# Query products as three rounded passes in one bank, grouped output weights added in transfer, weight checks over three stages

## The chip, the cores and the metric

The kernel runs on one core of a Trainium2 chip. The metric is the device time of one execution in microseconds; the kernel before takes 470.77 us, the median of three runs (470.35 to 471.19).

## The reference

Two layers on a batch of 2 × 512 rows of 512 values. Each of the four steps adds to its input and normalises over the row (layernorm). Cut to the first layer, which the change touches:

```python
q = (x @ Wq.T + bq).reshape(b, s, 32, 128)
sig_q = elu(q) + 1.0
q_sel = sig_q[:, :, ::4, :]                       # 8 of 32 heads are used
num = einsum('bshd,hde->bshe', q_sel, M)
den = einsum('bshd,hd->bsh', q_sel, z)[..., None] + 1e-6
out_heads = repeat(num / den, 4, axis=2)          # each head stands for 4
x = layernorm(x + out_heads.reshape(b, s, 4096) @ Wo.T)
xf = x / 128.0                                    # feed-forward, 1376 wide
inter = silu(xf @ w_gate.T) * (xf @ w_up.T)
inter_q = trunc(clip(inter * 128.0, -128.0, 127.0))
down = trunc(clip((inter_q @ w_down.T) * 128.0, -128.0, 127.0))
x = layernorm(x + down)
```

The feed-forward weights of this layer hold one magnitude with a sign, or zero. The second layer is a one-head attention and a gated feed-forward of the same width with ordinary weights.

## The kernel before, in words

**Stages.** Activations lie in eight row tiles of 128 × 512, four for each batch. The first layer has a query stage, a read stage, a gate-and-up stage and a down stage; the second follows.

**Query stage** (`queries`, L379). For each batch and each of 8 heads, `query_products` multiplies four 128-row blocks of the head's weights with the transposed rows in FP32 into one PSUM bank. ScalarE takes exp (L388) and relu (L390) from it, VectorE joins both into `q` (L392), of which sixteen stay in memory. Batch 0 goes first, head by head, then batch 1. The first product follows its rows tile by tile (`first_queries`, L368).

**Output weights.** As four output heads repeat one read head, their four 128 × 512 weight blocks can be summed. `wo` comes as two halves of two blocks for each head (L332) into six rooms of 512 KiB (`wop`). `sum_weights` (L404) adds the halves and then the two blocks, half of the heads on POOL and half on VectorE. `fold` (L412) multiplies the turned memory M with the sum; ScalarE writes the result, less its last column, to `mw` (L416, L417). The last column of `mw` holds `z`.

**Read stage** (`read`, L419). For each of eight row tiles, eight FP32 products of `q` with `mw` (L428) fill the eight PSUM banks. ScalarE takes the denominators (L432), VectorE inverts them; three heads leave over ScalarE (`y`, L441) and POOL (L445), five over VectorE (L450). The row tile is then normalised (`norm_a0`), cut into two rounded parts (`split`), and for batch 1 turned by squares and transfers.

**Weight checks.** To multiply with signs alone, the kernel divides the gate and up weights by their largest magnitude (`ternary`, ScalarE, L463) and counts on VectorE where sign times magnitude differs from the weight (`compare`, L210). There are 22 such checks (`check_up`): 15 from the fourth head of batch 1 on, seven in the first three tiles of the read stage. The sum (`total`, after the fourth tile) and the verdict (`verdict`, after the fifth) give a flag. TensorE loads it into a register (`branch`, L235) and each product of the next stage branches on it. For the products the weights are divided again into rooms of their own (`divided`), in the last six tiles of the read stage.

**Gate-and-up stage** (`up`, L604). For each batch and each of 11 chunks of the width, 16 rounded passes fill two banks (L611). ScalarE and VectorE turn them into the truncated middle values. Chunk c + 6 is divided when chunk c of batch 1 is through, into the room that this leaves (`to_divide`). The down weights are checked beside it in the same way, with POOL dividing (`check_down`, L465).

**Order.** Each engine has one instruction list; the framework orders it by its own estimates, `issue_after` pins single steps, and POOL's order is as written. Loads stand in SP's queue in the order written; a load whose room is in use holds up those behind it. `pair_tile` and `query_tile` rooms are reused by later stages.

Of the kernel before, what the change touches and what calls it, by code (L numbers as in the profile page):

```python
# [19 lines left out]
P = 128  # L20
# [12 lines left out]
LENT = 3  # L33
TOP12 = -4096
# [4 lines left out]
def kernel(  # L39
# [179 lines left out]
    def verdict(tot, sc, name):  # L219

        k = sc.shape[-1]
        pf = psum(f"pf_{name}")
        nc.tensor.matmul(pf[:, :1], ones, tot, start=True, stop=True)
        yes = small.tile([P, 1], F32, tag="yes", name=f"yes_{name}", bufs=1)
        nc.vector.tensor_scalar(yes, pf[:, :1], 0.0, None, ALU.is_equal)
        no = small.tile([P, 1], F32, tag="no", name=f"no_{name}", bufs=1)
        nc.vector.tensor_scalar(no, pf[:, :1], 0.0, None, ALU.not_equal)
        flag = const.tile([1, 1], I32, tag=f"flag_{name}", name=f"flag_{name}")
        nc.vector.tensor_copy(flag, yes[0:1, 0:1])
        eff = const.tile([P, k], F32, tag=f"eff_{name}", name=f"eff_{name}")  # L230
        nc.vector.tensor_scalar(eff, sc, yes, no, ALU.mult, ALU.add)
        return flag, eff
# [65 lines left out]
    wop = ctx.enter_context(tc.tile_pool(name="wop", bufs=6))  # L298

    def pair_tile(name):  # L300
        return wop.tile([P, 2, HID], F32, tag="wo", name=name)

    wqp = ctx.enter_context(tc.tile_pool(name="wqp", bufs=4))

    def query_tile(name):
        return wqp.tile([P, 2, HID], F32, tag="wq", name=name)

    with tc.tile_pool(name="a0w", bufs=1) as a0w, tc.tile_pool(name="a0", bufs=2) as a0:
# [12 lines left out]
        load_x(1)  # L321
# [4 lines left out]
        for h in range(NH):  # L326
            halves = []
            if h == 6:
                gus = up_weights(gu0_in, "0", range(1))
            for j in range(2):  # L330
                w = pair_tile(f"wo{h}_{j}")
                nc.sync.dma_start(w, wo0_in[h, :, ts(j, G // 2), :])  # L332
                halves.append(w)
            wos.append(halves)

        gus += up_weights(gu0_in, "0", range(1, len(CHUNKS)))
        nc.sync.dma_start(wqkv, wqkv_in.rearrange("(k p) f -> p k f", p=P))
        bqk = const.tile([D, 3], F32, tag="bqk", name="bqk")
        nc.sync.dma_start(bqk, bqk_in)
        nc.sync.dma_start(bv, bv_in.to_broadcast([P, D]))  # L340
        nc.sync.dma_start(wo1, wo1_in)
        nc.sync.dma_start(bo, bo_in.to_broadcast([P, HID]))

        mw = a0w.tile([D, NH, HID], F32, tag="mw", name="mw")
        nc.gpsimd.tensor_copy(mw[:, :, LAST], z)

        def query_products(pq, xt, h, at):  # L350
            for k in range(NK):
                done = nc.tensor.matmul(  # L352
                    pq[:, at], wq[h][:, k, :], xt[:, k, at],
                    start=(k == 0), stop=(k == NK - 1),
                )
            return done

        def first_rows(xt, t):
# [5 lines left out]
            nc.scalar.copy(xt[:, :2, ts(t, P)], pt[:, :2])  # L364
            nc.vector.tensor_copy(xt[:, 2:, ts(t, P)], pt[:, 2:])
            return done

        def first_queries(pq, xt):  # L368

            done = first_rows(xt, 0)  # L370
            for t in range(NT):
                if t + 1 < NT:
                    with tc.issue_after(done.ins):
                        done = first_rows(xt, t + 1)
                with tc.issue_after(done.ins):
                    done = query_products(pq, xt, 0, ts(t, P))
            return done

        def queries(b, xt, h):  # L379

            pq = psum(f"pq_{b}_{h}")
            if b == h == 0:
                done = first_queries(pq, xt)
            else:
                done = query_products(pq, xt, h, slice(0, S))

            e = a0.tile([D, S], F32, tag="e", name=f"e_{b}_{h}")
            nc.scalar.activation(e, pq, AF.Exp, bias=bq[:, h : h + 1])  # L388
            r = a0.tile([D, S], F32, tag="r", name=f"r_{b}_{h}")
            nc.scalar.activation(r, pq, AF.Relu, bias=bq[:, h : h + 1])  # L390
            q = a0.tile([D, S], F32, tag="q", name=f"q_{b}_{h}", bufs=16)
            nc.vector.scalar_tensor_tensor(q, e, 1.0, r, ALU.min, ALU.add)  # L392
            qs[b].append(q)
            return done
# [9 lines left out]
        def sum_weights(eng, h):  # L404

            w, w1 = wos[h]
            eng.tensor_add(w, w, w1)
# [52 lines left out]
        def ternary(eng, out, w, factor):  # L460

            if eng is nc.scalar:
                eng.activation(out, w, AF.Copy, scale=factor)  # L463
            else:
                eng.tensor_scalar(out, w, factor, None, ALU.mult)  # L465

        counts = const.tile([P, 2 * len(CHUNKS)], F32, tag="counts", name="counts")

        def check_up(c, a):
            n = CHUNKS[c][1]  # L470
            w = gus[c][:, a].rearrange("p k i -> p (k i)")
            t = a0.tile([P, NK * P], F32R, tag="t", name=f"t_{c}_{a}")
            ternary(nc.scalar, t[:, : NK * n], w, inv_up[:, a : a + 1])
            junk = a0.tile([P, NK * P], I8, tag="junk", name=f"junk_{c}_{a}", bufs=1)
            i = 2 * c + a
            compare(
                junk[:, : NK * n], t[:, : NK * n].bitcast(F32), w,
                sc_up[:, a : a + 1], counts[:, i : i + 1],
            )

        checks = [(c, a) for c in range(len(CHUNKS)) for a in range(2)]
        qs = [[], []]
        xt = xtp.tile([P, NK, S], F32, tag="xt", name="xt_a00")
        with tc.issue_after(queries(0, xt, 0).ins):
            queries(0, xt, 1)
        for h in range(2, NH):
            queries(0, xt, h)
            if h == 4:
                sum_weights(nc.gpsimd, 0)
                turn_memory()  # L490
                sum_weights(nc.vector, 1)
            elif h == 6:
                xt1 = transposed(xs[1], "a01")
                sum_weights(nc.vector, 2)
        sum_weights(nc.gpsimd, 3)
        for h in range(NH):
            queries(1, xt1, h)
            if h == 0:
                sum_weights(nc.vector, 4)
                sum_weights(nc.gpsimd, 5)  # L500
                fold(0)
                fold(1)
                with tc.issue_after(copies[-1].ins):
                    mx_up = largest(
                        [gus[0][:, a].rearrange("p k i -> p (k i)") for a in range(2)], "up"
                    )
            elif h == 1:
                top_up = over_partitions(mx_up, "up")
            elif h == 2:
                sc_up, inv_up = scales(top_up, "up")  # L510
                fold(2)
                fold(3)
                sum_weights(nc.vector, 6)
                sum_weights(nc.gpsimd, 7)
            elif h == 3:
                fold(4)
            elif h == 5:
                fold(5)
                fold(6)
            elif h == 6:  # L520
                fold(7)
            if h >= 3:
                for _ in range(3):
                    check_up(*checks.pop(0))
        order = [(b, t) for b in range(B) for t in range(NT)]
# [11 lines left out]
        def divided(c, a):  # L537
            n = CHUNKS[c][1]
            if c not in ts_up:
                t = (pair_tile if c in PAIRED else query_tile)(f"tu_{c}").bitcast(F32R)  # L540
                ts_up[c] = t.rearrange("p a (k i) -> p a k i", k=NK)
                if n < P:
                    nc.gpsimd.memset(ts_up[c][:, :, :, n:].bitcast(F32), 0.0)
            ternary(nc.scalar, ts_up[c][:, a, :, :n], gus[c][:, a], inv_up[:, a : a + 1])

        PAIRED = (LEAD - 2, LEAD - 1, len(CHUNKS) - 1)
        ts_up, x2 = {}, []
# [5 lines left out]
        for i, (b, t) in enumerate(order):  # L553
            steps = read(b, t, lambda steps: norm_a0(i - 1, steps) if i else None)
            for _ in range((3, 2, 2, 0, 0, 0, 0, 0)[i]):
                check_up(*checks.pop(0))
            if i == 3:
                tot_up = total(counts, "up")
            elif i == 4:
                flag_up, eff_up = verdict(tot_up, sc_up, "up")  # L560
            if i >= len(order) - LEAD:
                for a in range(2):
                    divided(i - len(order) + LEAD, a)
# [30 lines left out]
    with tc.tile_pool(name="f0", bufs=2) as f0:  # L594
        ternary_up = branch(flag_up)
        silu_scale = const.tile([P, 1], F32, tag="silu_scale", name="silu_scale")
        nc.vector.tensor_scalar(silu_scale, eff_up[:, 0:1], 1.0 / 128.0, None, ALU.mult)
# [6 lines left out]
        def up(b, c, behind=()):  # L604
            n = CHUNKS[c][1]
            t = ts_up[c]
            pp = [psum(f"pg_f0{b}_{c}"), psum(f"pu_f0{b}_{c}")]
# [33 lines left out]
            for part in to_divide.get((b, c), ()):  # L641
                divided(*part)
# [83 lines left out]
        step = up(1, 0)  # L726
        with tc.issue_after(step.ins):
            mx_d = largest([wds[0]], "down")
        up(1, 1)
        last = len(CHUNKS) - 1  # L730
        for c in range(LEAD, last + 1):
            up(0, c)
            if c == LEAD:
                top_d = over_partitions(mx_d, "down")
# [586 lines left out]
```

## Time and profile before

| | |
|---|---|
| median of three runs | 470.77 us (470.35 to 471.19) |
| profiled execution, first to last instruction | 468.7 us |
| median less that span | 2.1 us |
| query stage, to the first read product | 0 to about 72 us |
| read stage | 72 to 130.65 us |
| gate-and-up stage, to the first down product | 130.65 to 208.4 us |
| ScalarE busy, 24.5 to 72.3 us | 32.95 of 47.8 us |
| VectorE busy, 24.5 to 72.3 us | 30.68 of 47.8 us |
| transfers, 4.6 to 24.5 us | 356 GB/s, 98% of the engines' time |
| `wo` load, 512 KiB, issue to landing | 6.9 us (median of 16) |

The profiled execution's own time is known as its span; what lies around it is the difference in the third line. PE is TensorE's products, PEld its weight loads, DVE VectorE, ACT ScalarE, POOL GpSimd and SP the queue that issues most loads. A row of the view in order of time gives the start, the length, the engine, the line, the operation with output and inputs, the shape and the count. The length of consecutive instructions of one kind overlaps, so the distance from start to start is their rate. A bracket at the end names idle time before it and what ended that.

### The profile page before, as it was taken

The numbers are of one execution on the slowest core, as the hardware profiler recorded it, in microseconds if no ns is written. First come the engines' busy times: TensorE is split into PE (matmuls) and PEld (weight loads), VectorE is DVE, ScalarE is ACT, GpSimd is POOL, SyncE is SP. The second block draws the span as 40 slices with busy tenths as digits, with TensorE's granted clock in tenths as the row PEclk, the third lists the DMA queues.
The fourth block names the chain that finished last, engine by engine and source line by source line (L and its number), as shares of the span: only waits on it lengthen the run. The fifth ranks groups of instructions, "written<-read, shape, count | busy, mean of one in ns | idle before, by whom it ended". The sixth has DMA issues, their size and how long they took to land.

```text
span 468.7 us, 5727 instructions
## 1 busy us (share of the span) xinstructions
PE 461.0 (98%) x1883; PEld 329.0 (70%) x1883; DVE 329.5 (70%) x627; ACT 267.5 (57%) x507; POOL 115.1 (25%) x144
## 2 busy tenths in 40 slices
PE   9999999999999999999999999999999999999994
PEld 8454444434478888888866567888888888888884
DVE  1165677767876767775979889895755778998632
ACT  3344799557756767456756842584645768443101
POOL 0235101566543053600357032000000000050111
PEclk9999999999999999999999999999999999999999
DMA  8989900000006500051390000000000000001001
GB/s 284 381 297 363 387 9 0 0 0 3 1 1 134 201 1 3 11 162 45 91 390 31 0 1 1 1 0 1 1 0 1 0 1 1 1 24 45 37 31 45
DMA packets 21651, 35.02 MB, mean 75 GB/s; under 512 B 9840, under 2 KB 10736, under 8 KB 21616
## 3 DMA queue, kind: packets, MB, share of 16 engines
q1 hardware_dynamic: 19616, 33.73, 20.7%
q10 hardware_dynamic: 1872, 0.56, 0.5%
q8 instruction: 22, 0.36, 0.3%
q0 software_dynamic: 128, 0.26, 0.3%
q14 instruction: 13, 0.11, 0.1%
HBM read 31.40 MB, written 2.10 MB: 71 GB/s over the span
## 4 chain that ended last, share of the span: by engine, by line
PE 71%; ACT 7%; DVE 5%; issue 3%; POOL 0%; POOLq 0%; DVEq 0%; ACTq 0%
PE pm L1111 17%; PE pg_f L611 9%; PE pu_f L611 9%; PE pc L1111 8%; PE pdm L1199 7%; PE pd_f L666 4%; PE pdc L1199 4%; DVE x L450 3%; PE pqk L893 3%; PE po L428 2%; ACT y L441 2%; ACT t L463 2%; PE pv L906 2%; PE pot L989 1%; PE po L1005 1%
## 5 line engine op out<-in xcount | busy, mean ns | idle before, releaser
L428 PE MATMUL po<-mw,q 128*128 128x512 f32 x128 | 57.1, 598 | 0.3 <-DVE mv_a L139 0.2
L352 PE MATMUL pq<-xt_a,wq 128*128 128x512 f32 (+1 forms) x152 | 56.9, 526 | 0.0
L145 POOL TENSOR_TENSOR rstd_f<-mv_f,ln_eps 128x1 f32<-128x1 f32 x15 | 4.4, 293 | 169.3 <-DVE mv_f L1214 130.2
L428 PEld LDWEIGHTS po<-mw,q 128*128 128x128 f32 x128 | 22.9, 189 | 32.1 <-issue 17.7
L352 PEld LDWEIGHTS pq<-xt_a,wq 128*128 128x128 f32 x152 | 26.2, 190 | 27.4 <-issue 25.7
L1111 PE MATMUL pm<-r,ugu 128*128 128x512 f32 x152 | 37.7, 389 | 0.0
L1111 PE MATMUL pm<-r,it_early 128*128 128x512 f32 x144 | 36.7, 392 | 0.0
L1111 PEld LDWEIGHTS pm<-r,ugu 128*128 128x128 f32 x152 | 28.5, 188 | 5.9
L1111 PEld LDWEIGHTS pm<-r,it_early 128*128 128x128 f32 x144 | 27.0, 188 | 6.1 <-issue 0.5
L169 ACT ACTIVATE ta_f<-y_f,below_half 128x512 int8<-128x512 f32 (+1 forms) x22 | 15.9, 721 | 27.0 <-DVE y_f L157 26.7
L450 DVE SCALAR_TENSOR_TENSOR x<-po,den,x 128x511 f32<-128x511 f32 x40 | 29.8, 745 | 1.9
L1121 DVE SCALAR_TENSOR_TENSOR ev_q<-pm,ev_q 128x512 f32<-128x512 f32 x27 | 18.6, 688 | 14.4 <-PE pm L1111 14.4
L637 DVE SCALAR_TENSOR_TENSOR it_f<-tb_f,ta_f 128x512 fp32r<-128x512 int16 (+1 forms) x22 | 15.4, 702 | 18.3 <-ACT tb_f L170 18.3
L445 POOL TENSOR_TENSOR y<-y,y 128x511 f32<-128x511 f32 x16 | 20.3, 1271 | 31.5 <-ACT y L441 30.8
L388 ACT ACTIVATE e<-pq,bq 128x512 f32<-128x512 f32 x16 | 11.1, 692 | 24.1 <-PE pq L352 20.6
L611 PE MATMUL pg_f<-xh,tu 128*128 128x512 f32 x88 | 24.3, 398 | 0.0
L1120 ACT ACTIVATE ev_q<-pc 128x512 f32<-128x512 f32 x27 | 16.0, 593 | 14.2 <-PE pc L1111 14.1
L465 POOL TENSOR_SCALAR td<-wd,inv_down 128x512 fp32r<-128x512 f32 x11 | 18.2, 1668 | 22.1 <-DVE inv_down L205 22.1
L611 PE MATMUL pg_f<-xl,tu 128*128 128x512 f32 x88 | 23.6, 390 | 0.0
L611 PE MATMUL pu_f<-xh,tu 128*128 128x512 f32 x88 | 23.5, 389 | 0.0
L611 PE MATMUL pu_f<-xl,tu 128*128 128x512 f32 x88 | 23.5, 389 | 0.0
L1001 ACT ACTIVATE x<-x,off_f,rstd_f 128x512 f32<-128x512 f32 x7 | 5.7, 816 | 27.7 <-POOL off_f L1000 27.7
(315 smaller groups left out, 1087.5 us busy)
## 6 DMA issues: line engine op xcount, KB each, us to landing
gu<-in_gu SPq DMA_DIRECT2D x20, 512.0 KB, 7.9
wo<-in_wo SPq DMA_DIRECT2D x16, 512.0 KB, 6.9
wd<-in_wd SPq DMA_DIRECT2D x20, 256.0 KB, 4.5
wq<-in_wq SPq DMA_DIRECT2D x8, 256.0 KB, 4.9
x<-in_x SPq DMA_DIRECT2D x7, 256.0 KB, 5.4
out<-x SPq DMA_DIRECT2D x7, 256.0 KB, 2.0
wqkv<-in_wqkv SPq DMA_DIRECT2D x1, 768.0 KB, 10.8
xt_f<-squares SPq DMA_DIRECT2D x9, 64.0 KB, 2.4
```

What stands on the lines that cost most here:

```text
L169: nc.scalar.activation(a[:n], y, AF.Relu, bias=below_half[:n])
L352: done = nc.tensor.matmul(pq[:, at], wq[h][:, k, :], xt[:, k, at], start=(k == 0), stop=(k == NK - 1),)
L428: nc.tensor.matmul(po, qs[b][h0 + j][:, ts(t, P)], mw[:, h0 + j, :], start=True, stop=True,)
L445: nc.gpsimd.tensor_add(ys[0][:, :LAST], ys[0][:, :LAST], y[:, :LAST])
L450: steps.append(nc.vector.scalar_tensor_tensor(x[:, :LAST], four[j][:, :LAST], d, x[:, :LAST], ALU.mult, ALU.add))
L465: eng.tensor_scalar(out, w, factor, None, ALU.mult)
L611: nc.tensor.matmul(pp[a], t[:, a, i % NK, :], x2[b][i], start=(i == 0), stop=(i == 2 * NK - 1),)
L666: nc.tensor.matmul(pd, inter[b][c][:, ts(t, P)], td[c].bitcast(F32R), start=(c == 0), stop=(c == last),)
L1111: nc.tensor.matmul(p, w, x, start=(left[id(p)] == begun[id(p)]), stop=(left[id(p)] == 1))
L1120: nc.scalar.activation(ev, pc, AF.Copy, scale=CROSS)
L1121: nc.vector.scalar_tensor_tensor(ev, pm, MAIN, ev, ALU.mult, ALU.add)
L1199: nc.tensor.matmul(p[:, :w], got[j // 4][1][kind][:, j % 4], down_parts[j][kind][:, cols], start=(j == 0 and kind == kinds[0]), stop=(j == ...
```

## The change

The fifteen query products after the first are made from rounded parts. Weights and rows are each cut into an upper part and a rest, and a third pair carries the crossed terms at 4096 times smaller scale. Upper and rest passes (8) fill a bank, ScalarE multiplies that bank by 4097 in place (`raise_main`), and four crossed passes then add to the same bank. exp is taken in place in PSUM. The heads go in another order: 1 to 3 of batch 0, 1 to 3 and 0 of batch 1, then 4 to 7 with both batches in turn. The parts lie in rooms that are still unused: those of gate chunks 4 to 10, of `y`, `t`, `wos`, two spare tiles and both `xt` tiles.

Only the first half of each head's output weights is loaded by SP, now into four rooms; POOL issues a transfer of the second half that adds to it. `sum_weights` is one addition, always on VectorE. Gate chunks 0 to 3 are loaded ahead of the fifth head's output weights, chunks 4 to 10 after the last query product. In SP's list the loads for the second layer come out between the four gate chunks and the fifth head's output weights; batch 1's rows move ahead of the fourth head's query weights.

The checks take chunks 0 to 3 in the query stage, 4 to 6 in the read stage and 7 to 10 in the gate-and-up stage. For chunks below 6 the divided weights that are checked are those that are used. The counts are summed twice, with two verdicts: the first after the eighth read tile, where its product stands behind the last read product on TensorE, the second after chunk 6 of batch 0; chunks from 7 on branch on the second. In the gate-and-up stage batch 1's chunks 0 to 5 come in a row before chunk 6.

The order that results on the engines, as far as the prediction uses it: on ScalarE, a division of chunk 6 stands ahead of the last fold's output, and the divisions of chunks 4 and 5 and the second of chunk 6 stand among the first tile's denominators, ahead of its first `y`. On VectorE, the maximum of gate chunk 0 stands right after the third head's `q` and head 0's low weights, ahead of the fifth head's parts.

```diff
-        flag = const.tile([1, 1], I32, tag=f"flag_{name}", name=f"flag_{name}")
+        both = const.tile([P, k + 1], F32, tag=f"eff_{name}", name=f"eff_{name}")
+        flag = both[0:1, k : k + 1].bitcast(I32)
...
-    wop = ctx.enter_context(tc.tile_pool(name="wop", bufs=6))
+    wop = ctx.enter_context(tc.tile_pool(name="wop", bufs=4))
...
+    def spare_tile(name, dtype=F32):
+        return wop.tile([P, 2, HID], dtype, tag="wx", name=name, bufs=2)
...
+    def exact_weights(w, parts):
+        g, l, d = parts
+        nc.scalar.activation(g, w, AF.Copy, scale=UPPER / BIG)
+        nc.vector.scalar_tensor_tensor(l, g.bitcast(F32), -BIG, w, ALU.mult, ALU.add)
+        nc.vector.tensor_sub(d, l.bitcast(F32), g.bitcast(F32))
+
+    def upper_lower(src, h, m):
+        return (
+            nc.scalar.activation(h, src, AF.Copy, scale=UPPER),
+            nc.vector.tensor_sub(m, src, h.bitcast(F32)),
+        )
+
+    def crossed(d, h, m):
+        return nc.vector.scalar_tensor_tensor(
+            d, m.bitcast(F32), -BIG, h.bitcast(F32), ALU.mult, ALU.add
+        )
+
+    def raise_main(p):
+        return nc.scalar.activation(p, p, AF.Copy, scale=BIG + 1.0)
...
-        load_x(1)
+            elif h == 2:
+                load_x(1)
...
-            for j in range(2):
-                w = pair_tile(f"wo{h}_{j}")
-                nc.sync.dma_start(w, wo0_in[h, :, ts(j, G // 2), :])
-                halves.append(w)
-            wos.append(halves)
+            if h == 4:
+                gus = up_weights(gu0_in, "0", range(EARLY))
+            w = pair_tile(f"wo{h}")
+            nc.sync.dma_start(w, wo0_in[h, :, : G // 2, :])
+            wos.append(w)
...
+        def late_loads():
+            gus.extend(up_weights(gu0_in, "0", range(EARLY, len(CHUNKS))))
+            nc.sync.dma_start(wqkv, wqkv_in.rearrange("(k p) f -> p k f", p=P))
...
+        def first_rows(t):
...
-            nc.scalar.copy(xt[:, :2, ts(t, P)], pt[:, :2])
-            nc.vector.tensor_copy(xt[:, 2:, ts(t, P)], pt[:, 2:])
+            nc.scalar.copy(raw[:, :2, ts(t, P)], pt[:, :2])
+            nc.vector.tensor_copy(raw[:, 2:, ts(t, P)], pt[:, 2:])
+            lows.append(upper_lower(pt, high0[:, :, ts(t, P)], low0[:, :, ts(t, P)]))
...
+        def passes(p, b, h, kinds, start):
+            todo = [(wq3[h][i][:, ts(k, D)], rows3[b][i][k]) for i in kinds for k in range(NK)]
+            for i, (w, x) in enumerate(todo):
+                done = nc.tensor.matmul(
+                    p, w, x, start=(start and i == 0), stop=(i == len(todo) - 1),
+                    skip_group_check=not start,
+                )
+            return done
+
+        def main_queries(b, h):
+            pq = psum(f"pq_{b}_{h}")
+            passes(pq, b, h, (0, 1), True)
+            raise_main(pq)
+            return b, h, pq
+
+        def cross_queries(b, h, pq):
+            if (b, h) != (0, 0):
+                passes(pq, b, h, (2,), False)
+            r = a0.tile([D, S], F32, tag="r", name=f"r_{b}_{h}")
             nc.scalar.activation(r, pq, AF.Relu, bias=bq[:, h : h + 1])
+            nc.scalar.activation(pq, pq, AF.Exp, bias=bq[:, h : h + 1])
...
-            w, w1 = wos[h]
-            eng.tensor_add(w, w, w1)
+            w = wos[h]
...
+        for h in range(NH):
+            nc.gpsimd.dma_start(wos[h], wo0_in[h, :, G // 2 :, :], accum_op=ALU.add)
...
+        query_weights(1, lows[1])
+        items = [(0, 1), (0, 2), (0, 3), (1, 1), (1, 2), (1, 3), (1, 0)]
+        items += [(b, h) for h in range(NH // 2, NH) for b in range(B)]
+        held = (0, 0, pq)
+        checks = [(c, a) for c in range(EARLY) for a in range(2)]
+        SUMS = [5, 6, 7, 8, 10, 11, 12, 13]
+        FOLDS = [7, 8, 9, 10, 12, 13]
+        for i, (b, h) in enumerate(items):
+            begun = main_queries(b, h)
...
+            step = cross_queries(*held)
+            held = begun
...
+            elif 10 <= i < 14:
+                for _ in range(2):
+                    check_up(*checks.pop(0))
+        fold(6)
+        cross_queries(*held)
+        fold(7)
+        late_loads()
...
-            for _ in range((3, 2, 2, 0, 0, 0, 0, 0)[i]):
+            for _ in range((1, 1, 1, 1, 1, 1, 0, 0)[i]):
                 check_up(*checks.pop(0))
-            if i == 3:
-                tot_up = total(counts, "up")
-            elif i == 4:
+            if i == 6:
+                tot_up = total(counts_up[0], "up")
+            elif i == 7:
                 flag_up, eff_up = verdict(tot_up, sc_up, "up")
-            if i >= len(order) - LEAD:
-                for a in range(2):
-                    divided(i - len(order) + LEAD, a)
...
             for part in to_divide.get((b, c), ()):
-                divided(*part)
+                t = divided(*part)
+                if part in checks:
+                    checks.remove(part)
+                    junk = f0.tile([P, S], I8, tag="tr_a", name=f"junk_{part[0]}_{part[1]}")
+                    compare_up(*part, t, junk)
...
+        up(0, LEAD)
+        verdict_up = verdict(tot_up, sc_up, "up2")
+        for i in range(2, 4):
+            check_down(i)
+        up(1, LEAD)
+        decide(1, *verdict_up)
```

## The prediction

> **What bounds the kernel now.** The page comes first: its span and its busy times.
>
> ```profile
> span 468.7 us, 5727 instructions
> PE 461.0 (98%) x1883; PEld 329.0 (70%) x1883; DVE 329.5 (70%) x627; ACT 267.5 (57%) x507; POOL 115.1 (25%) x144
> ```
>
> TensorE is never idle for long, and the list of waits charges it with 0.2 us after the start. So the end moves by what TensorE does less, or waits more. The chain of waits names ScalarE and VectorE often before 118 us, but there they only just release what TensorE takes next.
>
> The second view is TensorE alone in order of time. The columns are start, length, line, operation and count; the length runs to the modelled end of the last matmul, so I use start to start.
>
> ```profile
> 25.32 7.03 PE L352 MATMUL pq<-xt_a,wq 128*128 128x512 f32 x16
> 32.19 1.91 PE L127 MATMUL pt_a<-ident,x 128*128 128x128 f32 x16
> ...
> 72.32 35.47 PE L428 MATMUL po<-mw,q 128*128 128x512 f32 x80
> ...
> 130.65 1.50 PE L611 MATMUL pg_f<-xh,tu 128*128 128x512 f32 x4
> ...
> 134.73 1.07 PE L611 MATMUL pg_f<-xh,tu 128*128 128x512 f32 x4
> 135.63 1.07 PE L611 MATMUL pg_f<-xl,tu 128*128 128x512 f32 x4
> 136.54 1.07 PE L611 MATMUL pu_f<-xh,tu 128*128 128x512 f32 x4
> ```
>
> Two query heads are 16 instructions (each FP32 product is two) from 25.32 to 32.19: 0.429 each, so four products cost 3.43 a head. A rounded pass of the same size (L611) starts four in 0.906: 0.227 each. Query stage: to 72; read stage (L428): to 130.65.
>
> Third view, ScalarE and VectorE in order of time, for spacing rather than duration:
>
> ```profile
> 56.20 0.67 ACT L388 ACTIVATE e<-pq,bq 128x512 f32<-128x512 f32 x1
> 56.77 0.67 ACT L390 ACTIVATE r<-pq,bq 128x512 f32<-128x512 f32 x1
> 57.34 0.17 ACT L416 ACTIVATE col<-pmw 128x1 f32<-128x1 f32 x1
> 57.39 0.72 ACT L463 ACTIVATE t<-gu,inv_up 128x512 fp32r<-128x512 f32 x1
> 58.00 0.69 ACT L417 ACTIVATE mw<-pmw,col 128x511 f32<-128x511 f32 x1
> ...
> 294.13 0.68 DVE L1165 TENSOR_TENSOR it_f<-ev,ev 128x512 f32<-128x512 f32 x1
> 294.73 0.68 DVE L1121 SCALAR_TENSOR_TENSOR ev_q<-pm,ev_q 128x512 f32<-128x512 f32 x1
> ```
>
> Back to back, ScalarE starts one with a bias every 0.57 and a scaling every 0.61; VectorE starts a two-input one every 0.60, though each is shown as 0.7.
>
> Fourth, the flag that TensorE loads before a branch (L235), and what comes before it:
>
> ```profile
> 204.14 0.41 PEld L223 LDWEIGHTS pf_down<-tot_down,ones 128*128 128x128 f32 x2
> 204.68 0.16 DVE L225 TENSOR_SCALAR yes_down<-pf_down 128x1 f32<-128x1 f32 x1 [1.30 <-PE pf_down L223]
> 204.87 0.14 DVE L229 CAST flag_down<-yes_down 1x1 int32<-1x1 f32 x1
> ...
> L235 PEldq SEQ_ASSERT  x2: 26/27/28, 131.2 to 205.7; - x2
> ```
>
> From the first weight load of the total to the end of the branch's register work is 205.7 − 204.1 = 1.6 us.
>
> **What the Trainium skill says.** "FP8 and Floating Point Precision", TensorE Precision Notes: true FP32 is four passes through the array, reduced precision is a truncated read. The trace agrees: 2 × 0.429 against 0.227 is 3.8 to 1. "ScalarE: Activation LUTs", Step-by-step, calls ScalarE's port to PSUM the faster one; no row of before writes PSUM from ScalarE. "Collectives: The Full Stack", The bandwidth ceiling, has an adding transfer read two sources and run at half rate (measured ratio 1.93); no such transfer runs in before.
>
> **The change part by part.**
>
> *Rounded passes.* 15 of the 16 head-and-batch products go from 8 instructions of 0.429 (3.43) to 12 of 0.227 (2.72). Saved: 15 × 0.71 = **10.7 us** of TensorE. The first keeps FP32. Laid end to end by hand in its new order from 11.0 us, where that first product ends, TensorE has 15 × 2.72 = 40.8, 24 transposes × 0.11 = 2.6, eight folds × 0.86 = 6.9 and 0.4 of small ones: the first read product comes at 61.7, not 72. On this line lie the times at which TensorE "asks" below. The crossed pass of an item waits for ScalarE's raise of its bank, but the next item's main passes (1.81) stand between, which cover a raise of 0.5 and its signals; uncovered, it would cost about 0.7 an item.
>
> *ScalarE, query stage.* 32 reads with bias × 0.57 = 18.2; 15 raises of a bank in place at 0.48 (four row cuts of L803 start from 294.78 to 296.69) = 7.2; 8 weight cuts × 0.53 (L803 to L809, 246.14 to 246.67) = 4.2; 8 row cuts × 0.48 = 3.8; first copies 1.5; memory 1.1; 8 folds × 0.62 = 5.0; 8 divisions × 0.61 = 4.9. Sum 45.9. TensorE needs about 50.7 from 11 us on, so ScalarE fits, 5 us to spare. A raise into PSUM is unseen: 0.40 to 0.69 bounds it, or −1 to +3 in the stage; I take 0.48.
>
> *VectorE, query stage.* 16 q, 16 weight parts, 16 row parts, 8 sums: 56 × 0.60 = 33.6; checks 8 × 0.86 (54.16 to 55.01) = 6.9; copies, maxima, scales 4.0. Sum 44.5. But 21 of these fall between 7 and 21 us. Laid in order at 0.60, the last low rows of batch 0 come at 11.6, the fourth crossed row at 15.2, the third head's low weights at 18.8 and batch 1's rows at 21.2. TensorE asks for them at 11.9, 15.6+, 19.1 and 21.6. That is only just hidden: +0.4 taken, 0 to +2.5. First rows: ScalarE cuts two tiles before it copies the third, and VectorE's fourth copy moves from 9.95 to 10.4: **+0.4**.
>
> *Grouped output weights.* Gone: POOL 4 × 2.42 and four of VectorE's pair sums (1.48 each); four POOL sums of 1.36 move to VectorE. Both kernels hide them under TensorE. The eight adding transfers are issued on POOL, each behind its first half; POOL has nothing else until the read stage. At 356 GB/s (the mean of 4.6 to 24.5 us) half a MiB takes 1.5, so two reads 2.9: an estimate from that page. SP has 4.5 MiB ahead of the first half of weight 0 and that itself, which at 200 and then 356 GB/s lands near 17; its add starts near 19. On SP, tiles 4 to 7 now stand behind four gate blocks and the loads for the second layer (1.3 MiB), and they also wait until sums 0 to 3 (34 to 41 us) free their rooms; each adds behind its load, so sum 4 is ready near 44 to 48 and sum 7 near 48 to 55. Folds 4 to 7 ask from 52 to 61. Hidden, with some 5 us ahead; without cover it costs one for one. VectorE's maximum of the first gate block stands early in its order, near 24 us; that block lands at 23 to 26 with adding traffic beside it. VectorE then stands up to 3 us, and the next thing late, the fifth head's parts, has that much.
>
> *Late loads.* Gate blocks 4 to 10 can only start when the last query head leaves their rooms, near 57.5. ScalarE's order puts a division of block 6 ahead of the last fold's output (needed by the eighth read product) and five more divisions ahead of the first y. Block 6 lands near 62.5 (SP issues block 5 first), the fold's output comes at 64 and is asked for at 67.7; the first y ends near 68.2 against 68.6. In before, the same corner holds 15 checks' tail: the read stage loses 58.3 − (128 × 0.429 + 1.75 + 0.28) = 1.4. Net **0**, −1 to +2.
>
> *Verdict moved to the eighth tile.* In before the flag was 20 us old. Now pf, the flag, its load and the branch stand behind the last read product: 1.6, less pf's own 0.27 paid either way, plus the branch and its restart, some 0.3: **+1.6** (1.2 to 2.6; VectorE's transpose of 0.7 may stand ahead).
>
> *Gate and up stage.* Eight comparisons (0.86) join VectorE, which is busy 54.8 of 77.4; divisions there existed. The second verdict's flag is ready about 1 us before TensorE, which has a whole chunk (3.63) between: 0, at most 1.5. Chunks 6 to 10 no longer alternate with batch 1's chunk that frees their room, which in before left TensorE 0.2 or so near 164 and 168; I count nothing for it. The down checks start about 5 us later; POOL's 11 × 1.67 = 18.4 from about 170 still end before the down products at 208.
>
> Sum: −10.7 + 0.4 + 0.4 + 0 + 1.6 = −8.3. The profiled span becomes 468.7 − 8.3 = 460.4; the runs' median lies 2.1 above the span, so 470.8 − 8.3 = **462.5**.
>
> **Rivals.** (a) *Adding transfers bind: slower.* In a row they end at 19 + 8T, and the last fold wants its sum by 60: free up to T = 5.1, then 8 us per us; from T = 6.2 on the gain is gone. At T = 8, 486. For: no row shows such a transfer, and POOL's queue is strictly in order. Against: half rate is 2.9. (b) *ScalarE or VectorE becomes the bound.* If the spacing were the shown 0.7 everywhere, ScalarE would need some 55 and the early VectorE list 2.5 more: 465 to 469.8, say 467.5. For: before already kept ScalarE full from 52 to 84 us. Against: measured spacing. (c) *No change:* the gain eaten by moderately late loads, 469.8 to 471.7. That passes are not rounded is excluded: L611 runs these types at 0.227.
>
> **How the numbers follow.** Forecast 0.60 (its own range 459 to 465), (b) 0.20, (a) 0.16, (c) 0.04. A measurement of this kernel tells 0.2%, or 0.9 us, from no change. Faster 0.80, same 0.04, slower 0.16. Forecast and (b) hold 0.80: 459.0 to 470.0.
>
> **What would show it.** Rounded query passes at 0.227 start to start; first read product near 62; ScalarE with short gaps in the query stage; a hole of about 1.6 between the last read product and the first gate product, released by VectorE's flag; the last sum waiting on no transfer. Wrong if TensorE waits in the fold on sums, if VectorE waits for the gate block beyond 29 us, or if the raise costs more than 0.7.

## The result, and the profile after

The changed kernel takes 463.04 us, the median of four runs (462.71 to 463.36), beside 470.85 for the kernel before in the same comparison: a ratio of 0.9836, with a 95% interval of 0.9822 to 0.985. The forecast was 462.5. The profiled span came out at 460.6 where 460.4 was forecast, but the profiled execution is the quickest of the four; the spans of the others are 460.9 to 461.3. The sum was right to about half a microsecond; several of its terms were not, and one of them, the adding transfers, has only 2.3 us of room left.

The page of the changed kernel, span and busy times:

```profile
span 460.6 us, 5889 instructions
PE 451.8 (98%) x1945; PEld 340.4 (74%) x1945; DVE 343.1 (74%) x663; ACT 271.4 (59%) x516; POOL 107.1 (23%) x144
```

TensorE is still the bound: its busy time fell by 9.2 us and the span by 8.1, although it runs 62 more instructions.

TensorE in order of time, changed kernel (start, length, line, operation, count):

```profile
11.29 1.20 PE L502 MATMUL pq<-xh_a,host_y 128*128 128x512 f32 x4
...
29.55 1.98 PE L502 MATMUL pq<-host,host_y 128*128 128x512 f32 x8
31.36 1.07 PE L502 MATMUL pq<-host,host_wos 128*128 128x512 f32 x4
32.27 1.07 PE L502 MATMUL pq<-xh_a,host_t 128*128 128x512 f32 x4
...
62.75 42.20 PE L557 MATMUL po<-mw,q 128*128 128x512 f32 x96
...
114.55 7.34 PE L557 MATMUL po<-mw,q 128*128 128x512 f32 x16
121.72 0.28 PE L224 MATMUL pf_up<-tot_up,ones 128*128 128x1 f32 x2
123.14 1.18 PE L735 MATMUL pg_f<-xh,tu 128*128 128x512 f32 x4 [1.14 <-ACT den L561]
```

Twelve query passes from 29.55 to 32.27 are 2.72 us, or 0.227 each. The first read product (L557) stands at 62.75 instead of 72.32. The first gate product stands at 123.14 instead of 130.65, so 2.06 of those 9.57 us are given back in the read stage. Behind it nothing moves by much: from the first gate product to the end it is 337.5 us instead of 338.1, or 0.6 less. Together: −9.57 + 2.06 − 0.6 = −8.1.

The other two views shown of before, for the changed kernel. First ScalarE in order of time, for the raise in place (L337) and exp in place (L521):

```profile
45.92 0.58 ACT L337 ACTIVATE pq<-pq 128x512 f32<-128x512 f32 x1
46.44 0.61 ACT L319 ACTIVATE host_y<-wq 128x512 fp32r<-128x512 f32 x1
46.96 0.67 ACT L520 ACTIVATE r<-pq,bq 128x512 f32<-128x512 f32 x1
47.53 0.65 ACT L521 ACTIVATE pq<-pq,bq 128x512 f32<-128x512 f32 x1
```

Back to back, the raise takes 0.52 from start to start, where 0.48 was assumed within 0.40 to 0.69. The exp in place keeps the spacing of before, 0.57, although its median length is 0.652 instead of 0.687 when it went to SBUF. That agrees in sign with the Trainium skill, "ScalarE: Activation LUTs", Step-by-step, which calls PSUM the lower-latency port; but back to back the step costs the engine the same here.

Then VectorE in order of time, and TensorE's register load, around the verdict:

```profile
122.04 0.16 DVE L226 TENSOR_SCALAR yes_up<-pf_up 128x1 f32<-128x1 f32 x1 [0.54 <-PE pf_up L224]
...
122.23 0.14 DVE L231 CAST eff_up<-yes_up 1x1 int32<-1x1 f32 x1
...
L237 PEldq TENSOR_LOAD <-eff_up x2: 318/403/488, 122.4 to 173.0; - x2
```

The first weight load of the verdict's product is at 121.30; the two weight loads and the product reach VectorE at 122.04; the flag is written by 122.37, loaded from 122.4, and the first gate weight is loaded at 123.13. The hole is 1.84 us. The second verdict's flag is loaded at 173.0; TensorE's products follow one another there without a gap.

### The profile page after: what moved, and what is told of

It reads as the page before. It is cut to its first block, busy times and chain, and to the rows that moved or that the text cites. A ratio compares the mean times of both kernels' runs of the same rounds, so it can differ in the third digit from the quotient of the medians.

```text
span 460.6 us, 5889 instructions
## 1 busy us (share of the span) xinstructions
PE 451.8 (98%) x1945; PEld 340.4 (74%) x1945; DVE 343.1 (74%) x663; ACT 271.4 (59%) x516; POOL 107.1 (23%) x144
## 4 chain that ended last, share of the span: by engine, by line
PE 92%; DVE 3%; issue 2%; ACT 1%; POOL 0%; POOLq 0%; DVEq 0%
PE pm L1244 17%; PE po L557 9%; PE pq L502 9%; PE pg_f L735 9%; PE pu_f L735 9%; PE pc L1244 8%; PE pdm L1332 8%; PE pd_f L794 4%; PE pdc L1332 4%; PE pqk L1026 3%; PE pv L1039 2%; PE pot L1122 1%; PE po L1138 1%; PE psc L1064 1%; PE pmw L543 1%
## 5 line engine op out<-in xcount | busy, mean ns | idle before, releaser
L557 PE MATMUL po<-mw,q 128*128 128x512 f32 x128 | 57.0, 598 | 0.6 <-ACT den L561 0.4
L557 PEld LDWEIGHTS po<-mw,q 128*128 128x128 f32 x128 | 22.9, 189 | 33.1 <-issue 18.6
L561 ACT ACTIVATE den<-po,den_eps 128x1 f32<-128x1 f32 x64 | 13.9, 278 | 12.5 <-PE po L557 12.4
L349 POOL TENSOR_SCALAR td<-wd,inv_down 128x512 fp32r<-128x512 f32 x11 | 19.8, 1821 | 2.0 <-DVE inv_down L206 2.0
L794 PE MATMUL pd_f<-td,it_f 128*128 128x512 f32 x88 | 20.3, 389 | 0.0
L735 PEld LDWEIGHTS pg_f<-xh,tu 128*128 128x128 f32 x88 | 16.1, 188 | 4.5 <-ACT den L561 1.2
## 6 DMA issues: line engine op xcount, KB each, us to landing
wqkv<-in_wqkv SPq DMA_DIRECT2D x1, 768.0 KB, 21.6
```

The lines of the kernel that those rows point to most:

```text
L557: nc.tensor.matmul(po, qs[b][h0 + j][:, ts(t, P)], mw[:, h0 + j, :], start=True, stop=True,)
L735: nc.tensor.matmul(pp[a], t[:, a, i % NK, :], x2[b][i], start=(i == 0), stop=(i == 2 * NK - 1),)
L794: nc.tensor.matmul(pd, inter[b][c][:, ts(t, P)], td[c].bitcast(F32R), start=(c == 0), stop=(c == last),)
```

## The experiments

All are variants of the changed kernel but one. Lines of a variant can differ by one or two from those of the changed kernel.

### Rounding alone undone

```diff
-            todo = [(wq3[h][i][:, ts(k, D)], rows3[b][i][k]) for i in kinds for k in range(NK)]
+            i, ks = (1, range(2)) if start else (2, range(2, NK))
+            todo = [(wq3[h][i][:, ts(k, D)].bitcast(F32), rows3[b][i][k].bitcast(F32)) for k in ks]
```

> The changed kernel with only the rounding of the query products undone: each of the 15 later products is four FP32 products again (two of them in the place of the eight main passes, two in the place of the crossed ones) on the same operands; all cuts, raises, sums and loads stay. It leaves out the rest of the exact product. My theory (TensorE sets the time of the query stage, and a product costs 8 x 0.429 = 3.43 us so instead of 12 x 0.227 = 2.72): +10.7 us over the changed kernel, 473.7 us, that is about 2.9 us slower than the kernel before (ratio 1.006), which is the whole price of everything else in the change. Rival (ScalarE, VectorE or a transfer already limits the changed query stage): part of the 0.71 us a product is hidden behind that limit, and the kernel is slower than the changed one by less than 9 us. Rival (the changed order of loads and sums brings a gain by itself): at or below the time of before.

Measured: 474.32 us (473.59 to 475.74), 1.0077 of the kernel before (1.0055 to 1.0099), 11.3 over the changed kernel. TensorE in order of time:

```profile
12.24 1.12 PE L503 MATMUL pq<-xl_a,host_y 128*128 128x512 f32 x2 [0.64 <-DVE xl_a L327]
...
73.95 2.31 PE L558 MATMUL po<-mw,q 128*128 128x512 f32 x5
```

From the first of the later products to the first read product it is 61.71 us, against 51.46 in the changed kernel: 10.25 more, of 15 × 0.71 = 10.65 reckoned. The wait of 0.64 ahead of them is of the variant's own making, as it asks for low rows where the changed kernel asks for high ones first. So TensorE's own work set the length of the query stage, and the rounding brings more than the whole gain. The rest of the change costs 3.6 us, or 3.0 without that wait, where +2.4 had been summed.

### The verdict one tile earlier

```diff
-            if i == 6:
+            if i == 5:
                 tot_up = total(counts_up[0], "up")
-            elif i == 7:
+            elif i == 6:
                 flag_up, eff_up = verdict(tot_up, sc_up, "up")
```

> The changed kernel with the first verdict listed after the seventh read tile instead of the eighth (its total after the sixth); nothing else. My theory: the 1.84 us between the first weight load of the verdict's product and that of the first gate product shrinks to about 0.4, the flag being old when TensorE loads it: 1.4 us faster than the changed kernel, about 461.6 us. Rival (the hole is TensorE waiting for the last read tile's banks to be emptied, since the profile names ScalarE's den as what released it): the hole stays, and the time is within 0.4 us of the changed kernel.

Measured: 461.73 us (461.2 to 461.98), 0.981 of before (0.9797 to 0.9824), 1.3 less than the changed kernel; the two ranges of times don't touch. TensorE in order of time:

```profile
62.46 42.18 PE L557 MATMUL po<-mw,q 128*128 128x512 f32 x96
...
113.35 0.28 PE L224 MATMUL pf_up<-tot_up,ones 128*128 128x1 f32 x2
...
117.36 4.53 PE L557 MATMUL po<-mw,q 128*128 128x512 f32 x10 [0.15 <-DVE mv_a L140]
121.32 1.48 PE L735 MATMUL pg_f<-xh,tu 128*128 128x512 f32 x4
```

The verdict's product lies among the eighth tile's work, and the first gate product follows the last read product with no hole. From the first read product (62.46) to the first gate product it is 58.86 us, 1.53 less than in the changed kernel. The profile had named a `den` of ScalarE as what released the gate product in the changed kernel; the run shows that it was the verdict, whose flag TensorE takes by a register load. This kernel is faster than both others.

### The late verdict alone, in the kernel before

```diff
-            if i == 3:
+            if i == 6:
                 tot_up = total(counts, "up")
-            elif i == 4:
+            elif i == 7:
                 flag_up, eff_up = verdict(tot_up, sc_up, "up")
```

> The kernel before with one edit: its total and verdict are listed after the seventh and eighth read tile instead of the fourth and fifth. My theory (a verdict right ahead of its branch costs the way over VectorE, memory and the branch once): 1.5 us slower than before (1.2 to 1.9), ratio about 1.003. Rival (the hole is the emptying of the last banks, and would be there with any verdict): within 0.4 us of before.

Measured: 472.96 us (472.29 to 473.03), a ratio of 1.0043 (1.0029 to 1.0056), 2.2 us slower, which is above the range expected. TensorE in order of time:

```profile
118.21 1.10 PE L428 MATMUL po<-mw,q 128*128 128x512 f32 x2 [0.72 <-DVE x L450]
...
124.70 7.34 PE L428 MATMUL po<-mw,q 128*128 128x512 f32 x16
131.88 0.28 PE L223 MATMUL pf_up<-tot_up,ones 128*128 128x1 f32 x2
133.29 1.19 PE L611 MATMUL pg_f<-xh,tu 128*128 128x512 f32 x4 [1.14 <-ACT den L432]
```

The last sixteen products of the kernel before, ahead of its gate product at 130.65:

```profile
123.89 7.33 PE L428 MATMUL po<-mw,q 128*128 128x512 f32 x16
```

From the last sixteen products to the gate product it is 8.59 us, as in the changed kernel (123.14 − 114.55 = 8.59), and 6.76 in before: the hole of 1.83 comes with the late verdict, without anything else of the change. Another 0.73 was lost earlier: the last sixteen products start 52.30 us behind the first read product (at 72.40) instead of 51.57. A wait for one of VectorE's `x` outputs stands there; which step of the new order put it there was not settled.

### The adding transfers left out

```diff
         for h in range(NH):
-            nc.gpsimd.dma_start(wos[h], wo0_in[h, :, G // 2 :, :], accum_op=ALU.add)
             if h == 0:
```

> The changed kernel without the eight adding transfers: the second half of the grouped output weights is left out of the sums. My theory (they are hidden, the last by a small margin: VectorE waits 1.4 us for two of them and TensorE for none): within 0.5 us of the changed kernel, 462.6 to 463.5. Rival (they bind, or slow the late loads of the gate blocks by standing in their way): 1.5 us or more faster than the changed kernel.

Measured: 463.05 us (462.5 to 463.8), the time of the changed kernel. What the transfers take shows in the windows of ten microseconds (the last two columns are the busy share of the 16 DMA engines and GB/s). Changed kernel, then the variant:

```profile
30.00:40.00 10.00, 10.00 (x42) 7.52 (x41) 6.51 (x11) 8.25 (x16) 0.00 (x0) 1.00 1.06 294
40.00:50.00 10.00, 10.00 (x41) 7.26 (x41) 6.18 (x15) 8.63 (x19) 3.43 (x4) 1.00 0.92 249
50.00:60.00 10.00, 10.00 (x42) 7.54 (x41) 8.99 (x20) 9.53 (x19) 0.00 (x0) 1.00 0.80 154
```

```profile
30.00:40.00 10.00, 10.00 (x43) 7.48 (x42) 6.55 (x10) 8.10 (x15) 0.00 (x0) 1.00 0.38 126
40.00:50.00 10.00, 10.00 (x42) 7.29 (x41) 6.92 (x16) 8.62 (x18) 0.00 (x0) 1.00 0.26 91
50.00:60.00 10.00, 10.00 (x42) 7.54 (x41) 8.65 (x19) 9.54 (x19) 0.00 (x0) 1.00 0.04 8
```

With 1.05 against 0.98 from 20 to 30 us, the shares differ by (0.07 + 0.68 + 0.66 + 0.76) × 10 = 21.7 us of all engines, or 2.7 us for each of the eight transfers. The forecast took 2.9, from two reads at 356 GB/s. The half rate comes from the Trainium skill, "Collectives: The Full Stack", The bandwidth ceiling, which speaks of reduce-scatter between cores and not of a load that adds. For such a load it proved near: 2.7 us beside 1.5 at 356 GB/s. But the transfers are hidden by little. VectorE's sums in the changed kernel, in order of time:

```profile
49.80 0.69 DVE L538 TENSOR_TENSOR wos<-wo 128x512 f32<-128x512 f32 x1 [0.90 <-DMA wo<-in_wo]
53.50 0.69 DVE L538 TENSOR_TENSOR wos<-wo 128x512 f32<-128x512 f32 x1 [0.46 <-DMA wo<-in_wo]
56.24 0.68 DVE L538 TENSOR_TENSOR wos<-wo 128x512 f32<-128x512 f32 x1
58.98 0.68 DVE L538 TENSOR_TENSOR wos<-wo 128x512 f32<-128x512 f32 x1
```

Sum 4 is ready at 50.49 and its fold starts at 52.85; sum 7 is ready at 59.66 and its fold starts at 61.90. The cover is 2.3 us, not 5.

### Four of them issued twice

```diff
+        for h in range(4, NH):
+            nc.gpsimd.dma_start(wos[h], wo0_in[h, :, G // 2 :, :], accum_op=ALU.add)
         query_weights(1, lows[1])
```

> The changed kernel with the adding transfers of output weights 4 to 7 issued a second time, after the first round (the second half of these four is then counted twice). My theory (the folds wait one for one once the last transfers are late; in the changed kernel the sum of 7 is ready 2.2 us before its fold): the four more transfers land about 2.9 us apart behind 58.4 us, at 61.3, 64.2, 67.1 and 70.0; fold 4, asked at 52.6, comes at 62.2 and the rest of the stage behind it: 9.5 us slower than the changed kernel (7 to 11), that is near 472.5 us. Rival (the transfers have much more room than they seem to, because the folds can slip behind the last query products): under 3 us slower than the changed kernel.

Measured: 474.47 us (473.52 to 475.32), 1.0074 of before (1.0057 to 1.0091), 11.4 over the changed kernel and just above the range expected. TensorE in order of time, then windows around the wait (length, busy time of PE, PEld, DVE, ACT and POOL, then the clock granted to TensorE as a share of its full speed, DMA share, GB/s):

```profile
61.76 2.08 PE L543 MATMUL pmw<-wos,m 128*128 128x512 f32 x2 [8.66 <-DVE wos L538]
62.85 2.69 PE L502 MATMUL pq<-xh_a,host_y 128*128 128x512 f32 x4
65.34 1.43 PE L502 MATMUL pq<-xl_a,host_y 128*128 128x512 f32 x4
66.60 1.07 PE L502 MATMUL pq<-host,host_x 128*128 128x512 f32 x4
67.51 1.02 PE L543 MATMUL pmw<-wos,m 128*128 128x512 f32 x2
```

```profile
52.90:61.70 8.80, 0.20 (x1) 0.00 (x0) 0.69 (x2) 1.83 (x4) 2.60 (x3) 0.67 1.06 209
61.70:65.30 3.60, 3.54 (x6) 2.17 (x7) 2.98 (x8) 1.36 (x3) 0.00 (x0) 0.50 1.07 212
65.30:67.50 2.20, 2.20 (x9) 1.79 (x8) 2.20 (x5) 0.70 (x2) 0.00 (x0) 0.82 1.07 212
```

Fold 4 comes 8.9 us later than in the changed kernel. Its last transfer lands at 60.99 instead of 49.77, 11.2 us later, and 2.3 of that were covered. The next 5.75 us (to 67.51) hold work that took 3.63 in the changed kernel (52.85 to 56.48): TensorE restarts at a granted clock of 0.50. So 2.1 us of the loss go with a lower clock after the idle stretch. The Trainium skill, "TensorE: Matmul & The Clock Gate", HAM oscillation, describes this: a wait longer than TensorE's activity window sends it back to half clock, and the next work starts slow. The 0.50 agrees. The page puts the window at about 3.4 us, but the kernel without crossed passes, below, lost clock around waits of 3.08 and 2.88 us, so a shorter wait can do it too.

### No raise, and two

```diff
             passes(pq, b, h, (0, 1), True)
-            raise_main(pq)
```

> The changed kernel without the 15 raises of a bank in place; the main passes then count with the wrong weight. My theory (ScalarE waits 8 us in the query stage and TensorE is full): within 0.5 us of the changed kernel. Rival (ScalarE, full from 43 to 59 us, already holds TensorE up): 1 us or more faster than the changed kernel.

Measured: 463.78 us (462.74 to 464.09): nothing gained, as expected of a ScalarE that holds nobody up. The time is 0.7 above the changed kernel, a little outside what was expected, but the ranges overlap.

```diff
             raise_main(pq)
+            nc.scalar.activation(pq, pq, AF.Copy)
```

> The changed kernel with a second ScalarE pass over each bank behind the raise (a plain copy in place, which changes no value). My theory (ScalarE has no gap from 43 to 59 us, where nine items fall; nine passes of 0.52 us are 4.7 us, less the 0.7 us that it waits right after): 3.5 us slower than the changed kernel (2 to 5), near 466.5 us. Rival (ScalarE's queue there is made of divisions that nobody waits for yet, so it can fall behind unseen): within 0.7 us of the changed kernel.

Measured: 463.05 us (462.65 to 463.33), no change at all. My theory fell here, and its rival held. The windows run to the first read product, in the changed kernel and in the variant (the fourth busy time is ScalarE's):

```profile
11.30:62.75 51.45, 51.45 (x224) 39.60 (x224) 39.15 (x72) 43.74 (x81) 7.65 (x9) 1.00 0.97 285
```

```profile
11.30:61.90 50.60, 50.60 (x221) 38.83 (x220) 38.26 (x70) 48.03 (x91) 8.43 (x9) 1.00 0.97 278
```

ScalarE is at 95% of the stage instead of 85%, and TensorE is full in both. The gapless stretch from 43 to 59 us that I had read as a limit was made of divisions which nothing waits for yet. With more work in the stage, the framework's plan set some of them later: the variant puts the last of the stage's eight divisions at 60.40, where the changed kernel has it at 56.30. It even lets the first read product (61.91) slip in ahead of the last four crossed passes (62.83).

### What binds next

The crossed passes, a third of TensorE's query work, are left out; in a second kernel the adding transfers as well.

```diff
-            if (b, h) != (0, 0):
+            if False:
                 passes(pq, b, h, (2,), False)
```

> The changed kernel without the crossed passes of the 15 products (a third of the rounded product is left out): TensorE has 15 x 4 x 0.227 = 13.6 us less to do in the query stage, and something else must decide there. My theory (the adding transfers come next: DMA is full from 4 to 57 us whatever TensorE does, and the last sum was ready at 59.7): the first read product moves from 62.75 only to about 60.5, and the kernel is 1 to 3 us faster than the changed one, about 461. Rival (ScalarE comes next: its work in the stage was 44.0 us busy): 5 to 8 us faster. Rival (nothing else is near): 13 us faster.

> The kernel without the crossed passes, and without the eight adding transfers as well (the second half of the grouped output weights is left out too). My theory: with the transfers away ScalarE decides the query stage, whose 44.0 us busy there leave 5 to 8 us of the 13.6: about 456.5 (455 to 458). Rival (ScalarE already decides with the transfers there): the same time as with them, within 1 us. Rival (TensorE alone decides): about 449.5.

Measured: 462.46 us (461.8 to 462.57) with the transfers, 451.29 us (451.21 to 451.47) without them. Taking 13.6 us of work from TensorE thus brings 0.6 us while the transfers are there, and 11.8 us when they are not. The two kernels from 30 to 60 us, with transfers first:

```profile
30.00:60.00 30.00, 22.94 (x72) 15.05 (x71) 16.04 (x33) 20.86 (x42) 3.43 (x4) 0.83 1.00 257
```

```profile
30.00:60.00 30.00, 28.33 (x94) 17.07 (x93) 23.21 (x49) 29.98 (x66) 1.96 (x2) 1.00 0.50 170
```

TensorE's long waits, in the first kernel and then in the second:

```profile
40.70 0.58 PE L202 MATMUL pbc_up<-dg_up,ones 2*128 2x2 f32 x2 [3.08 <-DVE dg_up L195]
52.84 2.08 PE L543 MATMUL pmw<-wos,m 128*128 128x512 f32 x2 [2.88 <-DVE wos L538]
```

```profile
50.90 1.12 PE L543 MATMUL pmw<-wos,m 128*128 128x512 f32 x2 [1.67 <-DVE wos L538]
```

In the first, the DMA share is 1.00 and every compute engine has gaps. TensorE waits 5.3 us for sums (1.4 of it just behind this window) and 3.08 for the gate weights' scale, which VectorE makes right behind a sum that had itself waited 1.80 us for its transfer. TensorE's clock is 0.83 on average. In the second some 2 us of the 13.6 are still missing. ScalarE is busy 29.98 of 30 us there, but the doubled raise has just shown that this alone makes no limit; TensorE's one wait in the window is for VectorE's last sum, which no transfer held up. Which of the two engines decides there was not tried. Both gains missed their ranges. With the transfers less was left than the 1 to 3 us expected, and the lost clock is part of it. Without them I had expected ScalarE to keep 6 to 9 us of the 13.6; the rival, that TensorE alone decides (449.5), was nearer. So in the query stage the adding transfers come next behind TensorE: taking away all 13.6 us brings 0.6 us, slow clock included. A smaller cut was not tried. What comes after the transfers, on ScalarE or VectorE, lies some 12 us below.

### Turned rows one block at a time

```diff
-            if i == 5:
+            if i == 4:
                 parts, block = split(0)
...
-            if i in (5, 6):
-                for k in range(2):
-                    block(2 * (i - 5) + k)
+            if 4 <= i < 8:
+                block(i - 4)
```

The early verdict is in this kernel too.

> The changed kernel with the verdict early, as in the earlier run of that edit alone, and the four blocks of the first batch's turned rows listed one behind each of the read tiles five to eight instead of two behind tiles six and seven. In the changed kernel two ScalarE casts in a row keep TensorE waiting 1.16 us near 108 us for the next den. My theory: a cast at a time costs less, and 0.5 to 1.0 us more are saved than by the early verdict alone: 460.7 to 461.2 us. Rival (the wait moves to another tile, since ScalarE has as much to do in all): within 0.3 us of the early verdict alone, 461.7.

Measured: 465.52 us (464.52 to 465.92), 0.9884 of before (0.9867 to 0.99), 3.8 slower than the early verdict alone. TensorE in order of time:

```profile
106.09 0.33 PE L275 MATMUL pt_f<-ident,x 128*128 128x128 f32 x1 [0.63 <-ACT x L665]
...
122.92 0.60 PE L275 MATMUL pt_f<-ident,x 128*128 128x128 f32 x4
123.67 0.95 PE L734 MATMUL pg_f<-xh,tu 128*128 128x512 f32 x3 [0.15 <-ACT y L570]
125.05 0.50 PE L734 MATMUL pg_f<-xh,tu 128*128 128x512 f32 x1 [0.43 <-ACT xh L280]
125.38 0.86 PE L734 MATMUL pg_f<-xl,tu 128*128 128x512 f32 x3
127.55 0.50 PE L734 MATMUL pg_f<-xl,tu 128*128 128x512 f32 x1 [1.31 <-DVE xl L281]
```

The fourth block now stands behind the last read tile, so ScalarE and VectorE cut it when the gate products already ask for it, behind the tile's own `den`, `y` and `x` steps. I had looked at one wait of 1.16 us and not at who asks for the moved step. The rival, a wait that moves elsewhere, was nearer, and even it was too mild.

## Why the prediction was right, and where it was not

**Rounded passes: right.** Reckoned −10.7; undone, the query stage is 10.25 longer. The first read product was forecast at 61.7 by laying the work end to end, or 62.5 with the two terms of +0.4, and came at 62.75. Of the 1.05 over 61.7, 0.29 lies ahead of the passes (11.29 instead of 11.0), the *First rows* step. The other 0.76 is no wait of TensorE for another engine, as the view of waits lists none from 11 to 63 us; where in TensorE's own work it lies was not told apart.

**ScalarE, query stage: the verdict right, the room too small.** The sum of 45.9 compares with 43.74 us busy from 11.3 to 62.75; four of its eight row cuts lie ahead of that. The raise costs 0.52 instead of 0.48. But "5 us to spare" counted the eight divisions as fixed; the doubled raise made ScalarE 4.3 us busier up to the first read product, and the kernel no slower. That refutes rival (b) for ScalarE; for VectorE it rests on the waits alone.

**VectorE, query stage: within its range.** +0.4 had been taken, 0 to +2.5, and no wait of TensorE for it shows there. The sign against it stayed away too: the gate block's maximum starts at 23.88, and not beyond 29 us.

**Grouped output weights: right in sign and in price, wrong in slack.** At 2.7 us for half a MiB against 2.9, the price of one transfer held. What failed is "sum 4 is ready near 44 to 48 and sum 7 near 48 to 55" and so "some 5 us ahead": they were ready at 50.5 and 59.7. I had let the first halves of 4 to 7 land at the rate of an empty DMA. They were issued from 32.33 us on, when the engines were full, and took 6.0 to 11.2 us: fold 4's landed at 43.6, POOL issued its adding transfer at 44.12, and it landed at 49.8. The loads for the second layer stood among them (the largest took 21.6 us to land); how much they cost was not tried apart. Rival (a) was priced as 19 + 8T, free to T = 5.1 us a transfer, as if all eight ran in a row from 19 us on; the last four began only at 44.12, and the measured room of 2.3 us leaves much less. The rival did not come true, but it is the nearest bound. Its price was also low: "one for one" leaves out the clock that TensorE loses while it waits.

**Late loads: within its range.** Between the first read product and the first gate product, the kernel with the early verdict takes 58.86 us, before 58.33: +0.5, where 0 (−1 to +2) was taken.

**Verdict moved to the eighth tile: right.** +1.6 was reckoned from the second flag's row; the hole is 1.84, and putting the verdict back saves 1.53 in the trace and 1.3 in the runs.

**Gate and up stage: right.** From the first gate to the first down product it is 77.5 us, and 77.58 before (to 208.23, not 208.4).

Rival (c) is out with the interval. The forecast was right for its reasons in the two terms that made it, −10.7 and +1.6. That the spans agree to 0.2 us is luck. Up to the first gate product 8.3 us were forecast and 7.5 gained. The missing 0.8 was nearly made up by 0.6 behind it, where nothing was counted, and most of that lies outside the change: from the issue of the last output transfer to the end it is 3.30 us instead of 3.75. Between the medians of the runs the gain is 7.8 us.

## What to carry to other kernels

A transfer that hides costs nothing only as long as its landing precedes its asker: set landing times against asking times, with the DMA's busy share in that window, before shortening the work that covers it. A full stretch of an engine is not a limit if what fills it can be moved, so ask of each instruction in it who waits. And a step moved later pays for the whole way to its reader, so list it one tile earlier than its result is used.

## What the runs showed of the hardware that was not expected

- After 8.66 us without work TensorE started again at a granted clock of 0.50, and the first four passes took 2.49 us to the start of the next group instead of 1.33. In the kernel without crossed passes, the granted clock stood at 0.50 from 38.96 to 45.79 and from 52.62 to 56.03, around waits of 3.08 and 2.88 us; the first drop came 1.3 us into its wait. From 30 to 60 us the mean was 0.83.
- POOL spends 0.86 us to issue an adding transfer of 512 KiB. The quickest landed 5.7 us after its issue; the three behind it landed 3.7, 2.5 and 2.5 us apart. In the kernel that issues four of them twice, the last seven landed 2.5 us apart, which is 210 GB/s.
- From the last weight load of the verdict's small product (121.73) to the first weight load behind the branch on its result (123.13) it took 1.4 us; the register load alone took 0.32 and 0.49 us in the two verdicts.
